# A down projection's first half in 98 block products instead of 112, with the inner factors made by GpSimd

## The chip, the cores and the metric

The kernel runs on one core of a Trainium2 chip. The core has a matrix engine (TensorE, "PE" in the profile; its weight loads are "PEld"), VectorE ("DVE"), ScalarE ("ACT"), GpSimd ("POOL") and SyncE ("SP"), which here issues nearly all DMAs. Each engine works through its own queue in order; the queues meet at semaphores. Matmuls write to PSUM, which VectorE and ScalarE can read and GpSimd in this kernel never touches. The metric is the device time of one execution in microseconds, as a median of several runs.

## What is computed

The input `x` has 8 sequences of 512 tokens of 512 features. All arithmetic is float32.

```
xn = layernorm(x)
q, k, v = xn Wq' + bq, xn Wk' + bk, xn Wv' + bv
s = ((elu(q)+1) * cumsum_over_tokens((elu(k)+1) * v) / sqrt(32)) Wo' + bo
h = silu(xn' Wgate' * scale) * (xn' Wup' * scale)     # xn' = Hadamard transform of xn * SU_ug
f = (Hadamard transform of h * SU_dp) Wdown' * scale   # 2048 -> 512
out = x + s * silu(f)
```

The Hadamard transforms and scales are folded into the weights at the start of the kernel.

## The kernel before

**Pairs, units, halves.** Sequences are taken two at a time (four pairs, p = 0 to 3). The two sequences of a pair are the two rows of a 2x2 block matrix product, and every projection is done with seven block products in place of eight (the Winograd form of Strassen's scheme). The seven factors are called P1 to P7 in the code; each operand tile has an axis of seven places for them. A pair runs attention (q, k, v and the output projection "o"), then the hidden layer in four units (u = 0 to 3, each giving a tile `ho` of 2x128 hidden features by 7 factors by 512 tokens), and after units 1 and 3 one half of the down projection: `down(p, 0, ...)` (units 0 and 1) and `down(p, 1, ...)` (units 2 and 3, which also gates and writes the output).

**Two levels in the hidden layer, one in down.** From the last unit of pair 0 on, the hidden units use the scheme twice (`by_blocks`, L947): for each of seven outer factors, `block_product` (L678) runs seven inner products, each of two matmuls of a 128x128 weight block with 256 tokens, into the PSUM banks px, py and pz. The outer sums a, v, u1, u3 and r are put together by VectorE and ScalarE as they read PSUM, and by two GpSimd additions (L961, L965). The down half has one level: `token_groups` (L568) makes 7 factors x 2 groups of rows x 2 blocks of 128 tokens x 4 contraction tiles, 112 products of 128 tokens with 256 output features.

**Closing a unit.** `gated` (L985) applies SiLU with ScalarE to the gate half, multiplies by the up half into `ho`, and forms the factors P4, P5, P6 and P7 for the next layer. In the units before a down half (`last`), the products for P7 and P2 and their subtractions are on VectorE, otherwise on GpSimd.

**Order.** The program's order is laid out by hand. `at(place, fn)` puts a step on an agenda in which one place is one product of a few matmuls; `advance` runs it. A block product takes its steps at places 0 (P1), 2 (P2), 3 (P7), 4 (P6), 8 (P5), 12 (P3), 13 (P4), and the next outer product begins at place 7, so two are always interleaved. Background work (normalizing later inputs, making weight factors) is put in with `later` and spread by `pace` behind evictions. A scheduler then fixes each engine's order at build time, by this order and by when it expects operands and buffers; `keep_in_program_order` pins an instruction behind the one that was written before it on its engine.

**Buffers.** `t8` has six tiles of 8 KB a partition for results, `hop` two for `ho` and `co`, `wpool` four for weights (asked for three ahead by `get_w`), and `xin` one tile for inputs, for reading normalized tokens back (`squares`) and for weight factors in the making. PSUM has three banks px, one py, two pz and two "t". `factors_kv` (L440) makes two-level factors of Wk and Wv for pairs 2 and 3, in `t8` tiles, during unit 1 of pair 1 and the down half behind it.

Of the kernel before, what the change touches and what calls it, by code (L numbers as in the profile page):

```python
# [8 lines left out]
F32 = mybir.dt.float32  # L9
# [6 lines left out]


P1, P2, P7, P3, P4, P5, P6 = range(7)


@with_exitstack
def kernel(
# [57 lines left out]
        tc.cur_priority = at  # L80

    nearest, urgent, idle = [], [], []

# [255 lines left out]
    def stream_w(name):  # L341
        w = new_w("%s_%s" % (name[0], name[1] if type(name[1]) is int else "%d_%d" % name[1]))
        if name[0] == "gu":
            u, i = name[1]
            nc.sync.dma_start(w, inner[u][:, i])
        elif name[0] == "kv":
            nc.sync.dma_start(w, inner["kv"][:, name[1]])
        elif name[0] == "down":
            h, i = name[1]
            assert wd_made[h] == 4  # L350
            w = by_factor(w, 4)
            nc.sync.dma_start(w, wd[h][:, i])
        else:
            nc.sync.dma_start(flat(w), kept["%s_%d" % name])
            if name[0] == "o":
                w = by_factor(w)
        return w
# [82 lines left out]
    def factors_kv(m, lo, hi):  # L440

        n = hi - lo
        if "kv" not in inner:
            inner["kv"] = dram.tile([P, 7, 2, 7, P], F32, tag="d_kv", name="d_kv")
        d = inner["kv"][:, lo:hi, ("k", "v").index(m)]
        t = t8.tile([P, 4, 4, P], F32, tag="t", name=f"f_{m}_{lo}")
        for g in range(2):
            nc.sync.dma_start(
                t[:, 2 * g : 2 * g + 2, :n],
                kept[f"{m}_{g}"].rearrange("p (j s e) -> p j s e", j=2, s=7)[:, :, lo:hi],  # L450
            )

        def store(c, o):
            nc.sync.dma_start(d[:, :, c, :], t[:, o, :n])

        def plain():
            for c, o in ((P4, 3), (P1, 0), (P2, 1)):
                store(c, o)

        def made(c, o, x, y, op):  # L460
            nc.vector.tensor_tensor(t[:, o, :n], t[:, x, :n], t[:, y, :n], op)
            store(c, o)

        def make():
            for c, o, x, y, op in (
                (P5, 3, 2, 3, ALU.add), (P7, 2, 0, 2, ALU.subtract),
                (P6, 0, 3, 0, ALU.subtract), (P3, 1, 1, 0, ALU.subtract),
            ):
                later(0.7, made, c, o, x, y, op)

        at(8, plain)
        at(14, make)


    agenda = []
# [199 lines left out]
        between()  # L675


    def block_product(name, w, x, out, add, done, time=0):  # L678


        px, py, pz = (bank(t, name, 2) for t in ("px", "py", "pz"))
        sums = {}

        def product(p, i, first):
            for lane in range(2):
                nc.tensor.matmul(  # L686
                    p[:, lane], w[:, lane, i, :], x[:, i, :],
                    start=(first and lane == 0), stop=True, skip_group_check=True,
                )

        def read(what, m, q):
            s = snap.tile([P, 2, H], F32, tag="s", name=f"{what}_{name}")
            if add is None:
                nc.scalar.copy(s, px)
            else:
                nc.vector.tensor_tensor(s, px, add[:, m, :, q], ALU.add)  # L696
            return s

        def output(o, s, p):
            pace(nc.vector.tensor_tensor(o, s, p, ALU.add), time if add is None else time / 2)  # L700

        def p1():
            product(px, P1, True)
            sums["a"] = read("sa", 0, 0)

        def p2():
            product(py, P2, True)
            output(out[:, 0, :, 0], sums["a"], py)

        def p7():  # L710
            product(pz, P7, True)

        def p6():
            product(px, P6, False)
            sums["b"] = read("sb", 1, 0)

        def p5():
            product(px, P5, False)
            sums["c"] = read("sc", 1, 1)
            output(out[:, 1, :, 1], sums["c"], pz)  # L720

        def p3():
            product(px, P3, False)
            if add is None:
                nc.scalar.copy(out[:, 0, :, 1], px)
            else:
                nc.vector.tensor_tensor(out[:, 0, :, 1], px, add[:, 0, :, 1], ALU.add)  # L727

        def p4():
            product(pz, P4, False)  # L730
            output(out[:, 1, :, 0], sums["b"], pz)
            if done:
                done()

        for place, fn in ((0, p1), (2, p2), (3, p7), (4, p6), (8, p5), (12, p3), (13, p4)):
            at(place, fn)
        advance(7)
# [147 lines left out]

    def fetch(name):
        t = t8.tile([P, NT, D], F32, tag="t", name=name)
        nc.sync.dma_start(t.rearrange("p n d -> p (n d)"), kept[name])
        return t


# [55 lines left out]
    def by_blocks(p, name, xo, weights, got, time=0):  # L947

        def new(what):
            return t8.tile([P, 2, 2, 2, H], F32, tag="t", name=f"{what}_{p}_{name}")  # L950

        def outer(i, out, add=None, done=None):
            block_product(f"{name}_{p}_{i}", weights(i), xo[:, i], out, add, done, time)

        ra = new("a")
        rest = {}

        def with_u1():
            rest["u3"] = r = new("u3")
            for m in range(2):  # L960
                nc.gpsimd.tensor_tensor(r[:, m], ru1[:, m], rv[:, m], ALU.add)  # L961

        def with_r():
            for m in range(2):
                nc.gpsimd.tensor_tensor(rv[:, m], rv[:, m], rr[:, m], ALU.add)  # L965
            got(rv, 1, 1)

        outer(P1, ra)
        rv, ru1 = new("v"), new("u1")
        outer(P5, rv)  # L970
        outer(P6, ru1, ra, with_u1)
        outer(P2, ra, ra, lambda: got(ra, 0, 0))
        rr = new("r")
        outer(P7, rr, ru1, with_r)
        while "u3" not in rest:
            advance(1)
        outer(P3, rest["u3"], rest["u3"], lambda: got(rest["u3"], 0, 1))
        outer(P4, ru1, rr, lambda: got(ru1, 1, 0))

    def hidden_unit(p, u, xo, ho, get_w, last, time=0):  # L980

        def sub(eng, c, a, b):
            eng.tensor_tensor(ho[:, :, c], ho[:, :, a], ho[:, :, b], ALU.subtract)  # L983

        def gated(t, a, s):  # L985
            eng = nc.vector if last and a != s else nc.gpsimd
            g, v = (t[:, :, lane].rearrange("p m q t -> p m (q t)") for lane in range(2))
            for m in range(2):
                nc.scalar.activation(g[:, m], g[:, m], AF.Silu, scale=col("w_gate", u + m * NU + a * NG))  # L989
            place = (P1, P7, P2, P3)[2 * a + s]  # L990
            eng.tensor_tensor(ho[:, :, place], g, v, ALU.mult)
            if place == P7:
                sub(eng, P5, P7, P1)
                sub(eng, P6, P3, P5)
                sub(eng, P7, P3, P7)
            if place == P2:
                sub(eng, P4, P2, P6)
# [3 lines left out]
    def down(p, half, hos, get_w, ds=None, ss=None, ys=None):  # L1001
# [43 lines left out]
        if half == 0:  # L1045
            for s in range(2):
                put_by(f"d_{p}_{s}", ds[s])

    def load_y(p, s):
        y = t8.tile([P, NT, D], F32, tag="t", name=f"y_{p}_{s}")  # L1050
# [169 lines left out]
    for p in range(B // 2):  # L1220
# [5 lines left out]
        for u in range(NU):  # L1226
# [5 lines left out]
                at_o = len(queue) - (2 if p == 0 else 0)  # L1232
                queue[at_o:at_o] = [(p, "o", 0), (p, "o", 1)]
            if u % 2:
                queue += [(p, "down", (u // 2, i)) for i in (P1, P7, P2, P6, P5, P3, P4)]
    ahead = []

    def ask(n):
# [107 lines left out]
    for p in range(B // 2):  # L1346
        if p:
            catch_up()
            inner_tokens(xo)
            co = hop.tile([P, 2, 7, L], F32, tag="h", name=f"co_{p}")  # L1350
        heads_made = (attention if p < 2 else attention_by_blocks)(p, xo, co, get_w)
        more = p + 1 < B // 2
        hos = []
        for u in range(NU):
# [9 lines left out]
            else:  # L1364
# [5 lines left out]
                    with background():  # L1370
                        normalized(3)
                ho = hop.tile([P, 2, 7, L], F32, tag="h", name=f"ho_{p}_{u}")
                hidden_unit(p, u, xo, ho, get_w, u % 2 == 1, 1.1 if p > 1 and u == 0 else 0)
                if u == 0:
                    heads_made()
                    project_out(p, co, get_w)
            hos.append(ho)
            late = 1 if p else 0
            if more and late <= u < 2 + late and (p, u) != (0, 1):
                with background():  # L1380
                    normalized(2 * p + 2 + u - late)
            if u == 1:
                if p == 0:
                    weights_ahead(NU - 1)
                    inner_tokens(xo, 6)
                if p == 1:
                    for i, (m, lo, hi) in enumerate((("k", 0, 4), ("k", 4, 7), ("v", 0, 4), ("v", 4, 7))):
                        at(2 + 12 * i, lambda m=m, lo=lo, hi=hi: factors_kv(m, lo, hi))
                flush()
                down(p, 0, hos, get_w)  # L1390
                hos = []
        flush()
        ds = [fetch(f"d_{p}_{s}") for s in range(2)]
        if more:
            catch_up()
# [57 lines left out]
```

## Time and profile before

| | |
|---|---|
| median of 3 runs | 1538.2 us (1536.04 to 1538.99) |
| the profiled execution | 1536.37 us, its span 1534.5 us, mean granted clock 0.997 |
| TensorE busy | 1513.9 us, 6092 records |
| VectorE / ScalarE / GpSimd busy | 1046.2 / 414.7 / 360.5 us |
| DMA | 288.93 MB, mean 188 GB/s |
| first down half of pairs 1, 2, 3 (start to end) | 627.96 to 678.89, 986.5 to 1037.5, 1344 to 1395 us |

A float32 matmul stands as two records in the trace, one behind the other, and their shown lengths overlap; what it costs is read from the distance of starts. "L584" is line 584 of the kernel. A line with shapes reads out<-in, and xN is the count. In a timeline, the bracket at the end of a line gives how long the engine sat idle before it and what ended that.

### The profile page before, as it was taken

How to read it: one execution, taken by the hardware profiler on the slowest of the kernel's cores; microseconds unless marked ns; L12 is line 12 of the kernel's file. 1: busy time of each engine (PE TensorE's matmuls, PEld its weight loads, DVE VectorE, ACT ScalarE, POOL GpSimd, SP SyncE). 2: the span in 40 equal slices, each digit the busy share in tenths (PEclk: the TensorE clock that was granted, in tenths of full speed). 3: DMA queues.
4: the chain of work that ended last, by engine and by line, in shares of the span. 5: the costliest groups of instructions: out<-in, count | busy, mean ns of one | idle time of the engine just before them, and what ended most of it. 6: DMA issues, size and time to landing. Idle time of an engine off the chain costs nothing.

```text
span 1534.5 us, 16212 instructions
## 1 busy us (share of the span) xinstructions
PE 1513.9 (99%) x6092; PEld 1154.2 (75%) x6092; DVE 1046.2 (68%) x1571; ACT 414.7 (27%) x668; POOL 360.5 (23%) x188
## 2 busy tenths in 40 slices
PE   7999999999999999999999999999999999999998
PEld 3446546747874688888885888888886888888887
DVE  8999788469777665636767895715675697633673
ACT  4462341232125411112115232111212332111211
POOL 1000000000320261205511235302621128200631
PEclk9999999999999999999999999999999999999999
DMA  8345778798975244784586644335484443525462
GB/s 275 96 149 170 237 273 238 228 300 280 271 282 141 96 145 176 239 275 164 167 269 217 188 144 162 116 119 182 172 247 154 142 144 113 185 93 183 160 259 81
DMA packets 213726, 288.93 MB, mean 188 GB/s; under 512 B 57488, under 2 KB 169360, under 8 KB 209424
## 3 DMA queue, kind: packets, MB, share of 16 engines
q1 hardware_dynamic: 213504, 287.87, 58.7%
q8 instruction: 48, 0.79, 0.2%
q14 instruction: 30, 0.25, 0.1%
q10 hardware_dynamic: 144, 0.03, 0.0%
HBM read 205.42 MB, written 82.44 MB: 188 GB/s over the span
## 4 chain that ended last, share of the span: by engine, by line
PE 82%; DVE 11%; DMA 4%; issue 1%; ACT 1%; POOL 0%; SPq 0%; POOLq 0%; DVEq 0%; ACTq 0%
PE px_gu L686 17%; PE px_dn L584 12%; PE pz_gu L686 9%; PE pz_dn L584 6%; PE py_gu L686 4%; PE py_dn L584 4%; PE px_kv L686 3%; PE px_o L584 3%; PE px_q L508 3%; PE px_gate L508 2%; PE pz_o L584 2%; PE pz_kv L686 2%; PE pz_q L508 2%; PE px_k L508 1%; PE px_v L508 1%
## 5 line engine op out<-in xcount | busy, mean ns | idle before, releaser
L686 PE MATMUL px_gu<-xo,w_gu 128*128 128x256 f32 x1456 | 348.4, 380 | 0.7 <-DVE sa_gu L696 0.6
L686 PEld LDWEIGHTS px_gu<-xo,w_gu 128*128 128x128 f32 x1456 | 275.2, 190 | 44.3 <-issue 2.4
L961 POOL TENSOR_TENSOR u_gu<-u_gu,v_gu 128x1024 f32<-128x1024 f32 x26 | 61.2, 2376 | 753.0 <-DVE u_gu L727 697.5
L584 PE MATMUL px_dn<-w_down,ho 128*128 128x256 f32 x1024 | 228.8, 379 | 0.9 <-DVE ho L93 0.9
L584 PEld LDWEIGHTS px_dn<-w_down,ho 128*128 128x128 f32 x1024 | 194.5, 190 | 29.4 <-issue 1.9
L686 PE MATMUL pz_gu<-xo,w_gu 128*128 128x256 f32 x728 | 187.4, 380 | 0.5 <-DVE u L524 0.4
L686 PEld LDWEIGHTS pz_gu<-xo,w_gu 128*128 128x128 f32 x728 | 137.6, 190 | 21.2 <-DVE a_gu L700 0.9
L584 PE MATMUL pz_dn<-w_down,ho 128*128 128x256 f32 x496 | 112.5, 379 | 0.6 <-DVE u L524 0.6
L584 PEld LDWEIGHTS pz_dn<-w_down,ho 128*128 128x128 f32 x496 | 93.8, 190 | 15.4 <-issue 1.2
L686 PE MATMUL py_gu<-xo,w_gu 128*128 128x256 f32 x364 | 93.7, 379 | 0.0
L1018 POOL TENSOR_TENSOR s<-s,d 128x512 f32<-128x512 f32 x30 | 40.0, 1332 | 166.0 <-ACT d L1017 166.0
L686 PEld LDWEIGHTS py_gu<-xo,w_gu 128*128 128x128 f32 x364 | 69.2, 190 | 9.4
L965 POOL TENSOR_TENSOR v_gu<-v_gu,r_gu 128x1024 f32<-128x1024 f32 x26 | 60.8, 2361 | 22.8 <-DVE r_gu L727 22.8
L508 PE MATMUL px_q<-xo,w_q 128*128 128x512 f32 x128 | 59.8, 593 | 0.3 <-ACT sa_q L520 0.3
L584 PE MATMUL px_o<-w_o,co 128*128 128x256 f32 x256 | 59.2, 380 | 0.3 <-DVE sa_o L595 0.3
L1017 ACT ACTIVATE d<-d 128x512 f32<-128x512 f32 x31 | 19.5, 630 | 144.9 <-DVE d L599 124.7
L584 PE MATMUL py_dn<-w_down,ho 128*128 128x256 f32 x256 | 57.9, 379 | 0.0
L989 ACT ACTIVATE a_gu<-a_gu,cols_sb 128x512 f32<-128x512 f32 x26 | 18.6, 720 | 142.2 <-DVE a_gu L727 140.8
L983 POOL TENSOR_TENSOR ho<-ho 128x1024 f32<-128x1024 f32 x24 | 56.3, 2357 | 1.4
L584 PEld LDWEIGHTS px_o<-w_o,co 128*128 128x128 f32 x256 | 48.3, 190 | 8.9 <-issue 1.0
L989 ACT ACTIVATE u_gu<-u_gu,cols_sb 128x512 f32<-128x512 f32 x52 | 36.6, 719 | 67.8 <-DVE u_gu L727 64.9
L584 PEld LDWEIGHTS py_dn<-w_down,ho 128*128 128x128 f32 x256 | 48.6, 190 | 6.6
(322 smaller groups left out, 2403.5 us busy)
## 6 DMA issues: line engine op xcount, KB each, us to landing
w_gu<-d_gu SPq DMA_DIRECT2D x91, 896.0 KB, 4.5
w_down<-d_down SPq DMA_DIRECT2D x56, 512.0 KB, 4.6
w_kv<-d_kv SPq DMA_DIRECT2D x14, 896.0 KB, 4.6
d_s<-o SPq DMA_DIRECT2D x8, 1024.0 KB, 6.3
d_d<-dn SPq DMA_DIRECT2D x8, 1024.0 KB, 7.4
d<-d_d SPq DMA_DIRECT2D x8, 1024.0 KB, 5.7
s<-d_s SPq DMA_DIRECT2D x8, 1024.0 KB, 8.7
y<-in_x_dram SPq DMA_DIRECT2D x8, 1024.0 KB, 7.6
```

What stands on the lines that cost most here:

```text
L508: nc.tensor.matmul(p.rearrange("p a t -> p (a t)") if len(r.shape) == 2 else p, ws[k][:, i, :], r, start=(first and k == 0), stop=(k == n ...
L584: nc.tensor.matmul(p[:, c], t[:, (2 * g + c) * P : (2 * g + c + 1) * P], ws[i](k), start=(first and k == 0 and c == cs[0]), stop=(k == n - ...
L686: nc.tensor.matmul(p[:, lane], w[:, lane, i, :], x[:, i, :], start=(first and lane == 0), stop=True, skip_group_check=True,)
L961: nc.gpsimd.tensor_tensor(r[:, m], ru1[:, m], rv[:, m], ALU.add)
L965: nc.gpsimd.tensor_tensor(rv[:, m], rv[:, m], rr[:, m], ALU.add)
L983: eng.tensor_tensor(ho[:, :, c], ho[:, :, a], ho[:, :, b], ALU.subtract)
L989: nc.scalar.activation(g[:, m], g[:, m], AF.Silu, scale=col("w_gate", u + m * NU + a * NG))
L1017: nc.scalar.activation(d, d, AF.Silu)
L1018: (nc.vector if final and (a, s) == (1, 0) else nc.gpsimd).tensor_tensor(r, r, d, ALU.mult)
```

## The change

For pairs 1, 2 and 3 the first half of down is done with two levels as well (`down_by_blocks`). Each of the seven outer factors now has seven inner products, and each of these adds two matmuls (the two feature blocks m of a unit) of a 128x128 weight block with 256 tokens: 7 x 7 x 2 = 98 products. Units 0 and 1 form the two rows of the inner contraction, the token halves its columns. The result comes out with features on partitions.

- The weights need a second level of factors: `factors_down` makes them once, in pair 1's attention, through the `xin` tile into DRAM (`dl`, 896 KB for each outer factor). `factors_kv` moves from unit 1 to places 118 to 163 of pair 1 and takes the `xin` tile too; the normalizing of sequences 4 and 5 moves to the beginning of pair 1.
- The inner factors of the activations are made by GpSimd: for each outer factor three subtractions on 128x512 (`factors`) and one after the P2 product (`last_factor`), all pinned to the written order. The first two sets begin in `gated` as soon as P3 is there.
- In the units before a down half, SiLU's result for P7 and P2 goes to a PSUM bank "t", and VectorE multiplies and subtracts from there, in 128x512 pieces; P6 and P4 go to GpSimd.
- The results are turned in 32x32 blocks by VectorE into the tile of unit 1's `ho` and stored as [token, feature] in eight DMAs a pair, four places apart (`store`), in runs of 32 elements. `fetch` reads that layout.

```
+    def factors_down(i):
+        if "dl" not in inner:
+            inner["dl"] = dram.tile([P, 7, 2, 7, P], F32, tag="d_dl", name="d_dl")
+        t = xin.tile([P, 3, 7, P], F32, tag="x", name=f"f_dl_{i}")
+        w = t.rearrange("p c s e -> p (c s e)")[:, : 2 * 7 * P].rearrange("p (m s e) -> p m s e", m=2, s=7)
+        for c in range(2):
+            for u in range(2):
+                nc.sync.dma_start(
+                    w[:, :, (P1, P2, P7, P4)[2 * c + u]], wd[0][:, i, 2 * u : 2 * u + 2, c * P : (c + 1) * P]
+                )
...
+                later(0.42, nc.vector.tensor_tensor, w[:, :, o], w[:, :, a], w[:, :, b], op)
...
+    def two_terms(w, x):
+        def product(p, i, first):
+            for k in range(2):
+                nc.tensor.matmul(
+                    p[:, 0], w[:, k, i, :], x(k, i),
+                    start=(first and k == 0), stop=(k == 1), skip_group_check=True,
+                )
+        return product
...
         def gated(t, a, s):
-            eng = nc.vector if last and a != s else nc.gpsimd
+            eng = nc.gpsimd
             g, v = (t[:, :, lane].rearrange("p m q t -> p m (q t)") for lane in range(2))
+            if last and a != s:
+                bs = []
+                for m in range(2):
+                    b = bank("t", f"g_{p}_{u}_{a}_{m}", 1)[:, 0]
+                    nc.scalar.activation(b, g[:, m], AF.Silu, scale=col("w_gate", u + m * NU + a * NG))
+                    if s:
+                        nc.vector.tensor_tensor(b, b, v[:, m], ALU.mult)
+                        nc.vector.tensor_tensor(ho[:, m, P5], b, ho[:, m, P1], ALU.subtract)
+                        bs.append(b)
+                    else:
+                        nc.vector.tensor_tensor(ho[:, m, P2], b, v[:, m], ALU.mult)
+                if s:
+                    in_order(sub(eng, P6, P3, P5))
+                    for m in range(2):
+                        nc.vector.tensor_tensor(ho[:, m, P7], ho[:, m, P3], bs[m], ALU.subtract)
+                else:
+                    in_order(sub(eng, P4, P2, P6))
+                return
...
+            if begin and place == P3:
+                begin()
...
+    def down_by_blocks(p, hos, get_w):
...
+        ORDER = (P1, P3, P6, P5, P7, P2, P4)
+        def factors(n):
...
+            in_order(nc.gpsimd.tensor_tensor(x, b(1, 1, o), b(0, 1, o), ALU.subtract))
+            in_order(nc.gpsimd.tensor_tensor(b(0, 1, o), b(0, 1, o), b(0, 0, o), ALU.subtract))
+            in_order(nc.gpsimd.tensor_tensor(y, b(1, 1, o), b(0, 1, o), ALU.subtract))
+            places[n] = {
+                P1: b(0, 0, o), P2: b(1, 0, o), P7: x, P6: y, P5: b(0, 1, o), P3: b(1, 1, o), P4: b(1, 0, o)
+            }
+        def last_factor(n):
+            b = block(1, 0, ORDER[n])
+            in_order(nc.gpsimd.tensor_tensor(b, b, places[n][P6], ALU.subtract))
...
+        def store(s, place):
+            z = h1[:, s, 0:4].rearrange("p c (i f) -> p c i f", f=32)
+            d = ds[s].rearrange("(i t) (c j f) -> j t c i f", t=32, j=4, f=32)
+            for j in range(4):
+                at(place + 4 * j, lambda j=j: nc.sync.dma_start(d[j], z[32 * j : 32 * j + 32]))
...
+        def begin():
+            room.extend(halves("r3"))
+            factors(0)
+            room.extend(halves("xy"))
+            factors(1)
+        def run():
+            at(4, lambda: factors(2))
+            for n in range(3, 7):
+                at(7 * n - 7, lambda n=n: factors(n))
+            for n in range(7):
+                at(7 * n + 3, lambda n=n: last_factor(n))
...
+            def plus(o, a, b):
+                o, a, b = (t.rearrange("p m l q t -> p (m l q t)") for t in (o, a, b))
+                nc.vector.tensor_tensor(o, a, b, ALU.add)
...
+            if p == 1:
+                with background():
+                    for b in (4, 5):
+                        normalized(b)
+                for n, i in enumerate(IN_TURN):
+                    at(40 + 11 * n, lambda i=i: factors_down(i))
+                for i, (m, lo, hi) in enumerate((("k", 0, 4), ("k", 4, 7), ("v", 0, 4), ("v", 4, 7))):
+                    at(118 + 15 * i, lambda m=m, lo=lo, hi=hi: factors_kv(m, lo, hi))
...
-                down(p, 0, hos, get_w)
+                if p:
+                    down_now()
+                else:
+                    down(p, 0, hos, get_w)
```

## The prediction

> **What bounds the kernel now.** I read the page's busy row first, then the chain, then the stage that the change rewrites, engine by engine.
>
> ```profile
> PE 1513.9 (99%) x6092; PEld 1154.2 (75%) x6092; DVE 1046.2 (68%) x1571; ACT 414.7 (27%) x668; POOL 360.5 (23%) x188
> PE 82%; DVE 11%; DMA 4%; issue 1%; ACT 1%; POOL 0%; SPq 0%; POOLq 0%; DVEq 0%; ACTq 0%
> ```
>
> TensorE is busy 99% of the span and carries 82% of the chain; GpSimd (POOL) is idle 77% of it. So time goes only if matmuls go, and comes back only where TensorE is made to wait. Next, a table by stretches over the first down half of pairs 1, 2 and 3, and TensorE's timeline in the first of them:
>
> ```profile
> 627.96:678.89 50.93, 50.93 (x237) 44.78 (x236) 21.88 (x31) 7.46 (x12) 2.00 (x1) 1.00 0.76 236
> 986.50:1037.50 51.00, 51.00 (x238) 44.82 (x237) 13.88 (x17) 7.46 (x12) 2.07 (x1) 1.00 0.39 125
> 1344.00:1395.00 51.00, 51.00 (x238) 44.80 (x238) 14.30 (x17) 7.50 (x13) 2.38 (x1) 1.00 0.38 119
> ...
> 635.73 1.46 PE L584 MATMUL px_dn<-w_down,ho 128*128 128x256 f32 x6
> 637.02 1.89 PE L584 MATMUL pz_dn<-w_down,ho 128*128 128x256 f32 x8
> 638.75 2.32 PE L584 MATMUL px_dn<-w_down,ho 128*128 128x256 f32 x10
> ...
> 654.72 17.43 PE L584 MATMUL px_dn<-w_down,ho 128*128 128x256 f32 x80
> 671.99 7.07 PE L584 MATMUL pz_dn<-w_down,ho 128*128 128x256 f32 x32
> ```
>
> The columns after the stretch are its length, then busy time (and count) of PE, PEld, DVE, ACT, POOL, then granted clock (1.00), DMA share and GB/s. All three stretches run TensorE without a gap; GpSimd has one instruction. A product leaves two records; the 80 records start 17.27 us before the next line, so a record is worth 17.27 / 80 = 0.216 us and a product 0.432 us. (The 380 ns of the page's groups overlap.) The three short lines show a second thing: six records of P1 run ahead of eight of P7 and the rest of P1 after them. The written order has P7's first. Whatever fixes TensorE's order at build time fills an expected wait with later work.
>
> GpSimd just before that stage, and its price for 512 elements:
>
> ```profile
> 622.09 4.68 POOL L965 TENSOR_TENSOR v_gu<-v_gu,r_gu 128x1024 f32<-128x1024 f32 x2 [2.13 <-DVE r_gu L727]
> 627.59 2.36 POOL L991 TENSOR_TENSOR ho<-v_gu 128x1024 f32<-128x1024 f32 x1 [0.83 <-ACT v_gu L989]
> ...
> L1018 POOL TENSOR_TENSOR s<-s,d x30: 1262/1267/1638, 419.3 to 1524.4; 128x512 f32<-128x512 f32 x30
> ...
> L991 DVE TENSOR_TENSOR ho<-u_gu x14: 1224/1312/1423, 399.3 to 1487.2; 128x1024 f32<-128x1024 f32 x14
> L983 DVE TENSOR_TENSOR ho<-ho x28: 1206/1212/1226, 400.8 to 1488.5; 128x1024 f32<-128x1024 f32 x28
> ```
>
> The reader should see that GpSimd is free from 629.95 on, that an operation on 128x512 takes 1.27 us (three figures: least, median, most), and that VectorE does twice the elements in 1.21 us.
>
> **The change part by part.**
>
> *Matmuls removed.* Now: 7 factors x 4 row blocks x 4 contraction tiles = 112 products, 48.4 us a pair. After: 7 outer x 7 inner x 2 terms = 98 of the same shape, 42.3 us. That is 14 x 0.432 = 6.04 us a pair, 18.1 us for three.
>
> *GpSimd's factors.* Each outer product needs four operations on 128x512: three in factors(), one in last_factor(). 28 x 1.27 = 35.5 us a pair, 5.07 us per outer product, against 14 x 0.432 = 6.04 us of TensorE. It keeps up by 0.97 us an outer product once it is ahead; the question is the start. Write a place as one product of two matmuls, 0.863 us, with place 0 at 627.96. Pinned order: the P3 product ends at 629.95; factors(0) gives x, the changed block and y at 631.2, 632.5 and 633.8. The first outer product wants x at place 3 (630.6) and y at place 4 (631.4): TensorE, if it kept the written order, would lose 0.7 and 1.7 us. factors(1) ends 637.6; P6, now on GpSimd, takes 2.36, to 639.9; last_factor(0) 641.2, wanted at 641.6 with the loss so far. factors(2) 645.0; P4, also moved, 647.4; last_factor(1) 648.6, wanted at place 20, 645.2 + 2.4 = 647.6: 1.1 more. factors(3) ends 652.4 against a want of 653.0, and from there GpSimd gains. So 3.5 us a pair is the most for the written order. Zero is the least: behind the first wait stand three products that need none of this (the last two of the unit and the next outer P1), 2.6 us, and the px6-pz8-px10 lines show such work being drawn forward. That row concerns a VectorE wait, though, and none shows a TensorE wait on GpSimd, so I take 1.5 us a pair, a little under the middle: 4.5 us.
>
> *VectorE against GpSimd.* Among new VectorE work only three additions (plus) per pair read two SBUF tensors; the gated products read PSUM. The row for L991 shows what an overlap costs: 1.40 us at 629.63, beside a GpSimd instruction, against 1.22 at 637.64. GpSimd's own L1018 goes from 1.27 to at most 1.64. Three additions of 1.22 us would hold GpSimd up by at most 3.7 us, after the third outer product, when it is 0.6 to 3.4 us ahead: 0 to 0.5 us a pair, taken as 0. [...]
>
> *The other VectorE work.* Per pair 37 evictions of 128x256 at 0.42 us (the L307 row's 419 ns), three additions at 1.22 and eight transposes at 0.68: 24.6 us (the whole stretch has 14 to 22 now, the unit's tail included). TensorE's 42 us covers it, and each PSUM bank is read with four places (3.45 us) to spare. P6 and P4 leave VectorE.
>
> *The gated products through PSUM, fourth unit too.* Activations 1.44 us, then six VectorE steps of 0.68 in place of 1.40 + 1.21 + 2.35: P7 is ready near 636 as now, and the early P1 and P7 products over the older unit cover it to 640.9. P4 would be ready at 641.3 and is wanted at 672. Nothing, up to 1 us a pair if that cover shrank.
>
> *Weights.* Seven loads of 896 KB for seven of 512 KB; the hidden units already take one 896 KB load (4.4 us) per 6.04 us. Nothing.
>
> *Stores.* Four transposes per token block, then eight stores of 256 KB in runs of 128 bytes, SP issuing them in turn with later weight loads behind, over 31 places (27 us) of the third unit. Nothing of before stores in such runs. The nearest row is the load z of the same shape: 4.0/6.1/7.7 us to land, and in the packet records 13 ns a packet alone, 20 in bursts. At 20 the 16,384 packets hold 16 engines 20 us, beside 15 us of work already there (DMA share 0.57 to 0.67 over 26 us): 35 us in 27, so loads slip up to 8 us. Weights are asked for three outer products ahead, 18.1 − 4.4 = 13.7 us of slack. Taken as nothing; it turns at 25 to 26 ns a packet. [...]
>
> *Pair 1's preparations.* Seven times, during attention: four loads of 128 KB, four VectorE operations at 0.42 and a store of 896 KB, all through the one xin buffer, with four factors_kv chains and two normalizations brought forward behind the same buffer. VectorE is busy 53 of 78 us there; 12 us of factors and one normalization (6 us) fit. A chain is about 4 + 2 + 6 us; five to seven end near 570 to 600, wanted from about 610. Bounds 0 to 4 us (SP or VectorE standing before a late buffer); I take 1, plus 0.3 a pair where halves join: 2.
>
> Sum: −18.1 + 4.5 + 2 = −11.6. Against the profiled execution (1536.37 = span 1534.5 + 1.87) that is 1524.8; the median of the three runs is 1.8 higher, so 1526.6. I say 1526.5.
>
> **Rivals.**
> *Everything is filled* (no wait survives): 1538.2 − 18.1 = 1520. For it, the gapless stretches; against, the zero margin at places 3, 4 and 20.
> *Most is lost in small waits*: written order kept (10.5), the VectorE additions (1.5) and 4 for pair 1: −2, so 1536; within 0.2% or just under.
> *GpSimd becomes the bound*, slower: it must do 28 operations and 4.72 us from 629.95. The old half ended at 678.9; with 1 us for the last product it decides at (678.9 − 629.95 − 4.7 − 1) / 28 = 1.54 us an operation. At 1.64, the most in the L1018 row, it ends 2.7 us later than now, 8 in all, 1546; with additions in the way 1552. Against: the median 1.27, and few two-input VectorE instructions nearby.
> *The 128-byte stores make weights late*, slower, if a packet takes over 28 ns: at 32, 33 + 15 − 27 − 13.7 = 7 us a pair, 1538.2 − 11.6 + 21 = 1548.
>
> **How the numbers follow.** Forecast 0.48 (its own range 1522 to 1532), filled 0.15, lost in waits 0.13, GpSimd 0.12, stores or late preparations 0.12. A measurement tells about 0.2%, 3 us, from no change. Faster: 0.48 + 0.15 + 0.08 = 0.71; same 0.05; slower 0.24. The range runs from 1519 (below the filled case) to 1543, leaving out the worse part of the two slow cases, some 0.17, and a little below.
>
> **What would show it.** The dl products in place of the dn ones: 196 records and 42.3 us a pair. Gaps on TensorE at the first px6 or pz7 and second pz4 of a dl stage, released by GpSimd, up to 3.5 us. GpSimd over 85% busy in that stage, its 128x512 median at 1.27; above 1.54 I am wrong about the sign. Stores landing in 6 us and gu weights still 4 to 5 us. If gaps stand instead around 480 to 620, the xin chain is the cause.

## Result and profile after

The changed kernel takes 1549.8 us (median), the kernel before 1537.1 in the same series: a ratio of 1.0085, 95% interval 1.0065 to 1.0105. The change makes the kernel slower, by 12.7 us; the forecast was 11.6 us faster. One execution of the changed kernel took 2264 us at a mean clock of 0.656 and is left out here, but not in the 1550.8 us from which the expectations below start. The profiled execution took 1549.79 us, its span 1548.0.

The page's busy row and the shares of the chain, of the changed kernel:

```profile
PE 1503.6 (97%) x6008; PEld 1140.0 (74%) x6008; DVE 1113.2 (72%) x1739; ACT 413.9 (27%) x680; POOL 508.9 (33%) x286
PE 78%; DVE 10%; POOL 4%; DMA 3%; issue 2%; ACT 1%; SPq 1%; POOLq 0%; DVEq 0%; ACTq 0%
```

84 records of TensorE are gone, which at 0.216 us is the promised 18.1 us. But TensorE fell from 99% to 97% of the span, and GpSimd, which had no share of the chain, has 4% of it. So the answer is in TensorE's waits. I counted them from the trace: wherever the start of one matmul follows the start of the one before by more than the 0.216 us of a 256-column record (0.432 for 512 columns), the excess is time in which TensorE stood or ran at a lower clock. The sum was 19.5 us before and is 51.4 now. 31.9 more, less 18.1, is 13.8; the span grew by 13.5. Where the excess lies:

```
excess over back-to-back matmuls, us
                              before   after
pair 1, 500 to 600 us           0.5      9.1   (one gap at 572)
pair 1, 600 to 650              0.0     10.4   (one gap at 611; start of the down half)
pair 1, 650 to 700              0.1      4.3   (down half)
pair 2's down half              0.2      5.6
pair 3's down half              0.0      4.3
all else                       18.7     17.7
```

Half of the loss lies before the rewritten products, in the stretch where the new weight factors are prepared. TensorE's waits from 555 to 620 us of the changed kernel (line, what it waited for: us in total, times, longest):

```profile
PE pz_gu L717 <- DVE u_gu L747: 5.6, 1, 5.6
PE px_gu L717 <- DMA w_gu<-d_gu: 5.3, 1, 5.3
```

The first, at 572.56, is a wait for an eviction on VectorE. Here is what VectorE did with the factors of Wd in that time, and below it GpSimd (start, duration, then the operation):

```profile
562.39 2.06 DVE L97 TENSOR_TENSOR f_dl<-f_dl 128x256 f32<-128x256 f32 x1
564.98 6.93 DVE L97 TENSOR_TENSOR f_dl<-f_dl 128x256 f32<-128x256 f32 x3
582.35 1.55 DVE L97 TENSOR_TENSOR f_dl<-f_dl 128x256 f32<-128x256 f32 x4
```
```profile
559.50 2.37 POOL L1057 TENSOR_TENSOR ho<-v_gu 128x1024 f32<-128x1024 f32 x1 [0.83 <-ACT v_gu L1055]
561.82 2.36 POOL L1057 TENSOR_TENSOR ho<-u_gu 128x1024 f32<-128x1024 f32 x1
564.25 7.37 POOL L1031 TENSOR_TENSOR ho<-ho 128x1024 f32<-128x1024 f32 x3
```

Seven sets of four small operations make these factors. The last set, from 582.35, does four in 1.55 us, beside no work of GpSimd. The four of the set before it take 2.06 us and three times 2.3 on average, a whole GpSimd operation each: while GpSimd ran one 2.36 us operation on two SBUF tensors behind another, each of these VectorE operations with two SBUF inputs got through once for one of GpSimd's. The eviction that TensorE needs is behind them in VectorE's queue.

The second gap, at 611.25, is a wait for a weight load. TensorE wanted the weights at 605.8; SP issued the load at 603.71, and it landed 7.5 us later instead of the usual 4.7. Here is SP's queue ahead of the load, and a table by stretches of the changed kernel (length, then busy time and count of PE, PEld, DVE, ACT, POOL, then granted clock, DMA share and GB/s):

```profile
596.88 3.01 SPq L462 DMA_DIRECT2D d_kv<-f_k  x4
599.93 0.54 SPq L930 DMA_DIRECT2D d_s<-o  x1
602.26 1.36 SPq L456 DMA_DIRECT2D f_k<-d_k  x2
603.71 0.59 SPq L349 DMA_DIRECT2D w_gu<-d_gu  x1
```
```profile
600.00:605.00 5.00, 5.00 (x25) 4.41 (x24) 1.29 (x2) 2.22 (x4) 0.00 (x0) 1.00 0.98 331
605.00:612.00 7.00, 1.71 (x7) 1.17 (x6) 0.72 (x2) 0.58 (x1) 0.00 (x0) 0.79 1.01 337
```

Two things come together. SP stood before stores of `factors_kv` (L462), whose VectorE steps were not done (2.8 us at the longest), and its next loads (L456, 1.7 us in two waits), and the weight load is behind them in its queue. And the DMA engines are full (shares of 0.98 and 1.01): results of attention, the stores and loads of `factors_kv` and weight loads share them. With the usual 4.7 us the load would have landed at 608.4, still 2.6 us late. The clock column shows a third thing: 0.79. After each of the two gaps TensorE's records start 0.427 us apart instead of 0.216, for 12 records after the first and 9 after the second. With that the gap at 572 costs 8.7 us (5.8 stood, 2.9 behind it) and the one at 611 7.8 (5.4 and 2.4).

The down halves themselves, in TensorE's timeline of pair 1 (the bracket is the idle time before, and what ended it):

```profile
646.25 1.13 PE L726 MATMUL pz_dl<-r_dl,w_dl 128*128 128x256 f32 x4 [0.53 <-POOL r_dl L1144]
648.95 1.13 PE L726 MATMUL px_dl<-r_dl,w_dl 128*128 128x256 f32 x4 [1.56 <-POOL r_dl L1146]
...
658.13 1.10 PE L726 MATMUL pz_dl<-ho,w_dl 128*128 128x256 f32 x4 [0.72 <-DVE a_dl L747]
...
665.42 1.13 PE L726 MATMUL pz_dl<-ho,w_dl 128*128 128x256 f32 x4 [1.44 <-POOL ho L1153]
```

From start to start, TensorE lost 0.69 and 1.73 us at the first two products that need a factor of GpSimd's, the same in all three pairs. The later two waits are pair 1's own: there the operations of `factors_kv` on VectorE run beside GpSimd's too, and both sides lose. A step of `factors_kv` (L469) took 2.24 us at 654.22, with the eviction for 658.13 behind it; GpSimd's timeline at that time is

```profile
653.10 2.81 POOL L1031 TENSOR_TENSOR ho<-ho 128x1024 f32<-128x1024 f32 x1
655.87 1.73 POOL L1153 TENSOR_TENSOR ho<-ho,r_dl 128x512 f32<-128x512 f32 x1
```

These and the operations at 650.20 and 658.90 (1.60 each) are 1.6 us longer together than 2.36 and 1.27 each, as much as the wait at 665.42.

A table by stretches of pairs 1 and 2, then operations of the down half with the least, median and most ns, then loads and stores of the page's last part (KB each, median us to landing):

```profile
639.74:684.00 44.26, 39.23 (x176) 32.56 (x174) 31.43 (x48) 8.29 (x18) 42.49 (x28) 1.00 0.67 208
998.00:1042.50 44.50, 41.69 (x182) 35.16 (x181) 24.23 (x43) 8.53 (x18) 42.65 (x30) 0.96 0.42 142
```
```profile
L1144 POOL TENSOR_TENSOR r_dl<-ho,ho x3: 1262/1262/1272, 644.9 to 1361.6; 128x512 f32<-128x512 f32 x3
L1197 DVE TENSOR_TENSOR r_dl<-r_dl,a_dl x3: 1237/1467/1870, 680.5 to 1394.3; 128x1024 f32<-128x1024 f32 x3
L1197 DVE TENSOR_TENSOR r_dl<-r_dl,u_dl x3: 1950/1954/1955, 682.0 to 1396.0; 128x1024 f32<-128x1024 f32 x3
```
```profile
w_gu<-d_gu SPq DMA_DIRECT2D x91, 896.0 KB, 4.7
w_dl<-d_dl SPq DMA_DIRECT2D x21, 896.0 KB, 4.6
d_d<-ho SPq DMA_DIRECT2D x24, 256.0 KB, 6.2
```

GpSimd is 96% busy, an undisturbed operation takes the 1.27 us foreseen, and weights and stores land in 4.6 and 6.2 us.

### The profile page after: what moved, and what is told of

It is laid out like the page before. It is cut to its first block, busy times and chain, and to the rows that moved or that the text cites. A ratio compares the mean times of both kernels' runs of the same rounds, so it can differ in the third digit from the quotient of the medians.

```text
span 1548.0 us, 16497 instructions
## 1 busy us (share of the span) xinstructions
PE 1503.6 (97%) x6008; PEld 1140.0 (74%) x6008; DVE 1113.2 (72%) x1739; ACT 413.9 (27%) x680; POOL 508.9 (33%) x286
## 4 chain that ended last, share of the span: by engine, by line
PE 78%; DVE 10%; POOL 4%; DMA 3%; issue 2%; ACT 1%; SPq 1%; POOLq 0%; DVEq 0%; ACTq 0%
PE px_gu L717 16%; PE pz_gu L717 8%; PE px_dn L620 8%; PE py_gu L717 4%; PE pz_dn L620 4%; PE px_o L620 3%; PE px_kv L717 3%; PE px_dl L726 3%; PE px_q L544 3%; PE px_gate L544 2%; PE py_dn L620 2%; PE px_up L544 2%; PE pz_o L620 2%; PE pz_kv L717 2%; PE pz_dl L726 2%
## 5 line engine op out<-in xcount | busy, mean ns | idle before, releaser
L620 PE MATMUL px_dn<-w_down,ho 128*128 128x256 f32 x640 | 143.0, 379 | 1.0 <-DVE ho L97 1.0
L620 PEld LDWEIGHTS px_dn<-w_down,ho 128*128 128x128 f32 x640 | 121.5, 190 | 19.6 <-issue 1.9
L1031 POOL TENSOR_TENSOR ho<-ho 128x1024 f32<-128x1024 f32 x38 | 90.0, 2375 | 25.0 <-DVE ho L1046 14.7
L726 PE MATMUL px_dl<-ho,w_dl 128*128 128x256 f32 x300 | 74.6, 385 | 1.5 <-DVE sc_dl L743 1.0
L620 PE MATMUL pz_dn<-w_down,ho 128*128 128x256 f32 x304 | 69.3, 380 | 0.3 <-DVE u L560 0.3
L726 PEld LDWEIGHTS px_dl<-ho,w_dl 128*128 128x128 f32 x300 | 57.6, 193 | 11.1 <-DVE sc_dl L743 2.3
L620 PEld LDWEIGHTS pz_dn<-w_down,ho 128*128 128x128 f32 x304 | 57.4, 190 | 10.6 <-issue 1.2
L1085 ACT ACTIVATE d<-d 128x512 f32<-128x512 f32 x31 | 19.5, 630 | 147.0 <-DVE d L635 127.3
L717 PE MATMUL px_kv<-xo,w_kv 128*128 128x256 f32 x224 | 53.6, 379 | 0.0
```

Of the source, the lines that this page charges most:

```text
L620: nc.tensor.matmul(p[:, c], t[:, (2 * g + c) * P : (2 * g + c + 1) * P], ws[i](k), start=(first and k == 0 and c == cs[0]), stop=(k == n - ...
L717: nc.tensor.matmul(p[:, lane], w[:, lane, i, :], x[:, i, :], start=(first and lane == 0), stop=True, skip_group_check=True,)
L726: nc.tensor.matmul(p[:, 0], w[:, k, i, :], x(k, i), start=(first and k == 0), stop=(k == 1), skip_group_check=True,)
L1031: return eng.tensor_tensor(ho[:, :, c], ho[:, :, a], ho[:, :, b], ALU.subtract)
L1085: nc.scalar.activation(d, d, AF.Silu)
```

## The experiments

The theory after the result: matmuls went as foreseen, and three separate things took more than they gave: (a) operations on VectorE with two SBUF inputs wait for GpSimd, which costs the gap at 572; (b) full DMA engines, which cost the gap at 611 (the runs below show another cause); (c) GpSimd's first factors come too late in each pair. The rivals: the gap at 572 is VectorE having too much to do at that place; (c) is hidden elsewhere; and the two large parts of the change, products through PSUM and factors on GpSimd, are themselves the loss. All edits are made on the changed kernel. It takes 1549.8 us; each series has its own runs of the kernel before, 1536.1 to 1537.3.

**encode_psum: one operand of each encode step through PSUM.**

```diff
+            nc.scalar.copy(b[:, 0], w[:, :, P4])
+            nc.scalar.copy(b[:, 1], w[:, :, P1])
-                later(0.42, nc.vector.tensor_tensor, w[:, :, o], w[:, :, a], w[:, :, b], op)
+            later(0.42, tt, w[:, :, P5], w[:, :, P7], b[:, 0], ALU.add)
...
```

> Only the seven encodes of the dl weights change: ScalarE first copies one operand of each subtraction to a PSUM bank, so that no VectorE instruction of them reads two SBUF tensors; place, count and sizes stay. Theory (GpSimd and a VectorE instruction with two SBUF inputs exclude each other): the f_dl instructions at 562 to 572 us fall from 2.0 to 2.6 us each to about 0.42, the 5.8 us gap of TensorE at 572 and the 2.9 us of slow matmuls behind it go, 1550.8 - 8.7 = about 1542. Rival (the set is simply late, by its loads or its place in VectorE's order): the instructions wait instead of lasting, the gap stays within 1 us, 1549 to 1552.

1545.3 us (1.0067, 1.0041 to 1.0093). The same number of VectorE operations, at about the same places; the set that made the gap stands at 567.00 to 569.61, beside GpSimd operations of 2.36 us as before. One of the two groups of the tile f_dl:

```profile
L97 DVE TENSOR_TENSOR f_dl<-t_e_dl,f_dl x14: 406/412/424, 497.7 to 581.1; 128x256 f32<-128x256 f32 x14
```

The longest is 424 ns, where the changed kernel has 2558. The gap at 572 is gone: from 500 to 600 us the excess is 1.0 instead of 9.1. That is (a), and not VectorE's load, since VectorE does the same work. The median fell by 4.5 us only, and the two intervals overlap, so the cause is shown by the trace and not by the time. Of the difference, 3.2 us are excess before 500 us, all of it ahead of the first instruction that differs (480 us). That is spread between executions, not a cost of the edit: over all the profiles here the excess ahead of 400 us varies by 3.9 us. The late weight load is still there, with a wait of 6.0 us.

**kv_moved: `factors_kv` later, out of the crowded stretch.**

```diff
-                for i, (m, lo, hi) in enumerate((("k", 0, 4), ("k", 4, 7), ("v", 0, 4), ("v", 4, 7))):
-                    at(118 + 15 * i, lambda m=m, lo=lo, hi=hi: factors_kv(m, lo, hi))
+                for i, (m, lo, hi) in zip((166, 182, 262, 280), (("k", 0, 4), ("k", 4, 7), ("v", 0, 4), ("v", 4, 7))):
+                    at(i, lambda m=m, lo=lo, hi=hi: factors_kv(m, lo, hi))
```

Its four steps are also issued one a place (`at(j, ...)`) in place of `later(0.7, ...)`.

> Only factors_kv moves: its four sets begin at places 166, 182, 262 and 280 of pair 1 in place of 118, 133, 148 and 163, and their VectorE work is issued at once, not behind evictions. Theory (the DMA engines are full at 590 to 612 us, with stores of o, stores of kv factors and loads of weights together, and a gu weight comes late): the 5.4 us gap at 611 and the 2.5 us of slow matmuls behind it go, and in pair 1's dl stage the waits beyond those of pair 2 (about 2 to 3 us) go: about 1540. Rival (the weight is late because SP stands before the xin buffer that the dl factors hold): the gap stays or moves by no more than 2 us, 1548 to 1552.

1553.4 us (1.0114, 1.0092 to 1.0137): a miss for the time. The table by stretches, and VectorE a little later:

```profile
600.00:605.00 5.00, 5.00 (x25) 4.24 (x24) 1.30 (x3) 1.76 (x3) 0.00 (x0) 1.00 1.02 348
```
```profile
635.57 2.10 DVE L469 TENSOR_TENSOR f_k<-f_k 128x384 f32<-128x384 f32 x1
637.59 0.68 DVE L743 TENSOR_TENSOR sc_gu<-px_gu,u_gu 128x512 f32<-128x512 f32 x1
638.20 2.65 DVE L469 TENSOR_TENSOR f_k<-f_k 128x384 f32<-128x384 f32 x1
```

TensorE has no gap around 611, so the gap comes from `factors_kv`. But (b) does not hold: the DMA engines are as full as before (1.02), and the two weight loads that SP issued at 598.60 and 599.09 took 6.7 and 8.4 us to land. What changed is the time of issue: 1.3 us after the first product behind the output projection, against 8.35 us in the changed kernel. Two of the kernels below say the same. This is how long the weight load took that TensorE waited for near that place, and the wait, in early_first and then in all_fixed (where the DMA share is 1.00 from 590 to 605):

```profile
DMA to landing us min/median/max: 5.9/5.9/5.9
PE px_gu L717 <- DMA w_gu<-d_gu: 3.9, 1, 3.9
```
```profile
DMA to landing us min/median/max: 9.4/9.4/9.4
PE px_gu L725 <- DMA w_gu<-d_gu: 1.0, 1, 1.0
```

A load that lands in 5.9 us is waited for when it is issued late, at 605.30; one that needs 9.4 us, issued at 592.74, costs 1.0. The gap at 611 is SP's queue standing before `factors_kv`; the full DMA engines only lengthen it.

Nor is time gained, for the moved operations now stand beside GpSimd, take 2.10 and 2.65 us in place of 0.55, and TensorE waits three times behind them, 4.8 us in all from 634 to 641. One wait was exchanged for another of kind (a).

**early_first: the first factors behind the unit's P1 product.**

```diff
-            if begin and place == P3:
-                begin()
+            if begin and place in (P1, P3):
+                begin((P1, P3).index(place))
...
+                elif begin:
+                    at(16, lambda: in_order(sub(eng, P4, P2, P6)))
```

`factors(0)` is given to GpSimd before the P3 product, `factors(1)` behind it. The subtraction that makes P4 is put off 16 places, and there it reads a P6 that its own last factor has already replaced: the P4 factor of this kernel, and of all_three, is another one than the reference's. Instructions and sizes are the same, so the time can be read.

> The first three GpSimd operations of a dl stage are written behind the P1 product instead of the P3 product, and the P4 subtraction sixteen places later. Theory (TensorE waits for x, y and the last factor only because GpSimd begins too late): the waits of 0.7 and 1.7 us at the first dl products go in all three pairs, with the slow matmuls behind them in pair 2: 2.5 to 4 us a pair, about 1541. Rival (GpSimd is the bound of the stage in any order): the wait moves to a later factor, and the time stays within 3 us of 1550.8.

1545.5 us (1.0065, 1.0040 to 1.0089). In pairs 2 and 3 the excess of the down half falls from 5.6 and 4.3 us to 2.5 each; the two waits on GpSimd are gone. What is left in pair 2:

```profile
PE px_dl L726 <- DVE sc_dl L743: 0.9, 1, 0.9
PE px_gu L717 <- DVE sc_gu L743: 0.8, 1, 0.8
```

The second stands behind the six gating operations on VectorE, the first behind an addition of two SBUF tensors (L1197), which takes 2.0 us beside GpSimd. So (c) holds, with 1.8 to 3.1 us a pair; the time, 4.3 us less, lies between theory and rival.

**gate_sbuf and factors_vector: each of the change's two large parts undone alone.**

```diff
-            eng = nc.gpsimd
+            eng = nc.vector if last and a != s else nc.gpsimd
...
-            if last and a != s:
+            if False:
```

> The changed kernel with one part undone: the gated products for P7 and P2 and their subtractions are on VectorE in SBUF, as in the kernel before. Theory of exclusion: six VectorE instructions a pair with two SBUF inputs now meet GpSimd's unbroken row of factors, each stands up to 1.3 to 2.4 us, and the evictions behind them are late: 3 to 6 us a pair, about 1560 to 1568. Rival (it is GpSimd's own load that counts, which loses 4.7 us a pair here): the first waits of the dl stage shrink, 1543 to 1548.

1559.3 us (1.0150, 1.0133 to 1.0167), with products and subtractions on SBUF tensors. The start of pair 2's down half, GpSimd, and what TensorE waits for:

```profile
1007.90 2.25 POOL L1144 TENSOR_TENSOR r_dl<-ho,ho 128x512 f32<-128x512 f32 x1
1010.22 2.13 POOL L1145 TENSOR_TENSOR ho<-ho 128x512 f32<-128x512 f32 x1
1012.43 2.12 POOL L1146 TENSOR_TENSOR r_dl<-ho,ho 128x512 f32<-128x512 f32 x1
```
```profile
PE px_dl L726 <- POOL r_dl L1146: 3.3, 1, 3.3
PE pz_dl L726 <- POOL r_dl L1144: 1.8, 1, 1.8
```

GpSimd's factors take 2.1 to 2.25 us in place of 1.27, and both starting waits grow. This part as a whole (PSUM, and P6 and P4 on GpSimd) is worth 9.6 us to the changed kernel.

```diff
-            in_order(nc.gpsimd.tensor_tensor(x, b(1, 1, o), b(0, 1, o), ALU.subtract))
+            in_order(nc.vector.tensor_tensor(x, b(1, 1, o), b(0, 1, o), ALU.subtract))
...
```

The other two and `last_factor` go to VectorE likewise.

> The changed kernel with the 28 operations of factors and last_factor on VectorE in place of GpSimd (P6 and P4 stay on GpSimd). If VectorE's load bounds the stage: 28 x 0.69 = 19.3 us on top of the 24.6 and the gating, some 50 us for 42 us of matmuls, 6 us or more a pair later, 1565 to 1575. Rival (VectorE does an operation in half the time, and nothing excludes anything): the waits for x, y and the last factor go and little replaces them, 1540 to 1546.

1567.7 us (1.0198, 1.0176 to 1.0219). VectorE is 40.0 of 44.5 us busy in pair 2's down half, against 24.2, and the waits move to its evictions:

```profile
PE pz_gu L717 <- DVE u_gu L747: 2.6, 1, 2.6
```

So neither large part is the loss; each is better as the change has it.

**all_three: the first three edits together.**

> The three edits together. If the three causes are separate and make up the loss, the gains add: 1550.8 - 8.7 - 11 - 9 = about 1522, below the kernel before. If they hide one another or a common limit stands behind them, less than two thirds of that, above 1532.

1541.2 us (1.0027, 1.0013 to 1.0040): better than each alone, and above what adding them up gave, since `factors_kv` at its new place brings its waits along (12.1 us of excess from 600 to 650, of it 5.3 in three waits from 631 to 641). That is the second of the two readings foreseen, above 1532.

**all_fixed: the steps of `factors_kv` through PSUM too, at places 258, 278, 298 and 318.** Here the P4 subtraction is put off by 9 places, ahead of the last factor.

```diff
+            nc.scalar.copy(b, t[:, 3, :n])
+            nc.scalar.copy(b2, t[:, 0, :n])
+            made(P5, 3, t[:, 2, :n], b, ALU.add)
...
+                    at(9, lambda: in_order(sub(eng, P4, P2, P6)))
```

> Three edits on the changed kernel: the encodes of the dl weights through PSUM; the four sets of factors_kv at places 258, 278, 298 and 318 of pair 1 (its third and fourth unit), their operands too through PSUM; the first three GpSimd operations of a dl stage behind the P1 product and the P4 subtraction nine places later, before the last factor of P6. Theory (exclusion of two-SBUF-input VectorE work and GpSimd, full DMA engines at 590 to 612, a late start of GpSimd): the gaps at 572 and 611 us go (-16), pair 1's dl stage waits no longer than the others, and 2.5 us a pair stay: 1550.8 - 16 - 4 - 5 = about 1526, below the kernel before. Rival (the preparations cost wherever they stand): the waits turn up at 680 to 760 us, and the time stays above 1534.

1533.7 us (0.9976, 0.9966 to 0.9986): faster than before, by 3.6 us, though not the 11 hoped for. The excess is 34.6 us, 15.1 over that of before: 0.7 from 500 to 600 us, 5.1 from 600 to 700, 2.6 and 2.5 in pairs 2 and 3, 2.2 from 700 to 850, and 3.1 more than the kernel before ahead of 500 us, which is no more than the spread between executions. In pair 1's down half three waits of 1.0, 0.8 and 0.8 us are left, all behind evictions on VectorE.

**all_plus: the additions (`plus`) as well, in halves with one operand through PSUM.**

```diff
-                nc.vector.tensor_tensor(o, a, b, ALU.add)
+                for m in range(2):
+                    nc.scalar.copy(c, b[:, m])
+                    nc.vector.tensor_tensor(o[:, m], a[:, m], c, ALU.add)
```

> all_fixed, and the three additions of a dl stage (plus) in halves of 512 whose second operand ScalarE has copied to PSUM. Theory of exclusion: the additions, 2.0 us each beside GpSimd in place of 1.22, fall to two of about 0.7, and the wait of 1.0 us late in each dl stage goes: 2 to 3 us below all_fixed. Rival (more instructions, more waits): the same or up to 2 us above it.

1540.3 us (1.0024, 1.0012 to 1.0036): a miss. In pairs 2 and 3 the excess fell as foreseen, 2.6 to 1.4. But in pair 1 a gap of 8.2 us opened at 725, in the hidden units behind the down half. SP's waits from 690 to 730 us, its timeline there, and TensorE's wait for weights from 550 to 780:

```profile
SPq L462 <- DVE f_k L469: 11.1, 2, 10.9
```
```profile
705.92 0.58 SPq L1177 DMA_DIRECT2D d_d<-ho  x1
717.45 2.15 SPq L462 DMA_DIRECT2D d_kv<-f_k  x4
719.68 0.47 SPq L349 DMA_DIRECT2D w_gu<-d_gu  x1
```
```profile
PE px_gu L725 <- DMA w_gu<-d_gu: 10.7, 3, 8.0
```

SP stood 10.9 us before a store of `factors_kv` whose VectorE step had not run, and a weight load was behind it in SP's queue: the same kind of gap as the one at 611 of the changed kernel. The next three kernels ask what that gap hangs on.

**best_paced, best_moved: the steps of `factors_kv` given room between evictions again; its four starts moved to 268, 286, 304 and 322.**

```diff
-            made(P5, 3, t[:, 2, :n], b, ALU.add)
+            later(0.7, made, P5, 3, t[:, 2, :n], b, ALU.add)
...
```

The other three steps likewise, and evictions in the third and fourth units of pair 1 are given such room; that is best_paced. best_moved changes the four places alone.

> All_plus (1540.3), with the encode steps of the attention weights given out one behind each eviction (room 0.7 us) instead of all at once, and with such room in units 3 and 4 of pair 1. Theory 'queue': the 8.2 and 2.2 us gaps at 725 to 740 come from SP standing 10.9 us before a store whose VectorE step was late, with the weight loads behind it; a step with room no longer piles up, but a store can still stand, so the sum stays uncertain: if the piling up was the cause, the gap goes and the time is 1528 to 1532. Rival 'late wherever': paced steps come later still, SP stands longer before their stores, and the gap stays or grows: 1540 or more.

> All_plus (1540.3), with the four preparations of the attention weights begun at places 268, 286, 304 and 322 instead of 258, 278, 298 and 318; nothing else changes. Theory 'queue': SP's wait before the store depends on where the VectorE step falls among evictions, gating and additions; 10 places (8.6 us) later for the first and 4 for the last move the last two further into the stage of pair 1 that has the additions, so a wait of SP comes again, of the size of the last one: 1536 to 1544. Rival 'position only': the gap was a chance meeting of one store with one weight load, and goes: 1529 to 1532.

1546.2 us (1.0061, 1.0044 to 1.0078) and 1541.9 (1.0030, 1.0018 to 1.0043). In both, SP stands before such a store again (6.7 and 7.4 us at the longest) and TensorE before a weight load for 6.4 and 7.5. Neither pacing nor a shift of 4 to 10 places cures it, as the rival of the first text and the theory of the second had said.

**plus_late: all_plus with pair 1's additions whole again.**

```diff
+                if p == 1:
+                    nc.vector.tensor_tensor(o, a, b, ALU.add)
+                    return
```

> All_plus with the additions of pair 1 back as one VectorE operation on two SBUF tensors each; the halves through PSUM stay in pairs 2 and 3. Pair 1 is then as in all_fixed (1533.7), whose SP had no wait over 5.1 us there, and pairs 2 and 3 lose 1.35 us each instead of 2.5. Theory 'the additions cost their own wait, and the 8 us of all_plus belong to pair 1 alone': 1533.7 - 2 x 1.15 = 1531.4. Rival 'the ScalarE copies of the halves cost somewhere of their own, in every pair': 1534 or more.

1530.3 us (0.9957, 0.9943 to 0.9971): the best of all, 5.8 us under the kernel before, and 1.1 under what was expected. The excess from 700 to 850 us is 1.6 instead of 18.0. So the gap belongs to the halved additions of pair 1 together with `factors_kv`; by which step of the planner they hold up the VectorE operation is open. Pair 1 pays for the whole additions with one wait of 2.0 us.

## Why the prediction was wrong

The forecast for the profiled execution was 1524.8 us, and it took 1549.8: 25 us to explain. By the terms of the sum:

- **Matmuls removed**, −18.1: exact, 6008 records for 6092.
- **Pair 1's preparations**, bounded 0 to 4 and taken as 2 with the joins: this step failed. The gaps at 572 and 611 cost 8.7 and 7.8 us. The step counted how long VectorE and the chain through xin would be busy, and that held (the 28 operations had all begun by 583.5 us). It did not ask which engine would run beside those operations; encode_psum shows that the gap at 572 was their two SBUF inputs. The gap at 611 is what the step itself named, "SP or VectorE standing before a late buffer", but its price was too low: SP stood before `factors_kv` while a weight load was behind it, and the slow clock came on top. So "the xin chain is the cause" was wrong for the first gap and near the truth for the second.
- **VectorE against GpSimd**, 0 to 0.5 a pair and taken as 0: this step failed too, in size and in reach. The row for L991 showed a loss of 0.18 us, where 0.32 us of the operations overlapped. The profile of before had a row with nearly the whole price that the forecast did not weigh; it stands below the list. Where GpSimd ran without a pause, VectorE operations with two SBUF inputs lost far more: 0.42 us became 2.0 to 2.6 beside GpSimd operations of 2.36, and the additions took 1.95 (L1197) against 1.22. With one operand in PSUM they took 406 to 424 ns beside the same operations of GpSimd (encode_psum). The forecast also counted only the three additions; the operations of factors_down and factors_kv, which are of the same kind, cost more.
- **GpSimd's factors**, 0 to 3.5 a pair and taken as 1.5: the working was right, the choice was not. It gave 0.7 and 1.7 us for the written order, and the trace has 0.69 and 1.73 in every pair; nothing was drawn forward into them. The third wait, 1.1 at last_factor(1), did not come in pairs 2 and 3; in pair 1 it was 1.6, by VectorE's disturbance. With 0.1 us behind each wait and 1.7 us of lower clock in pair 2, the starts cost 9.6 us for three pairs in place of 4.5. The row with px6, pz8 and px10 showed TensorE's work filled around a VectorE wait and was carried over to a wait on GpSimd, which no row showed.
- The rest of the down halves, 7.0 us in place of 0, is mostly evictions and factors behind such pairs of operations: 4.2 in pair 1, where `factors_kv` runs, 1.1 and 1.7 in the others.
- **Stores, weights, the products through PSUM, the GpSimd price**: right. 256 KB in runs of 128 bytes landed in 6.2 us, at 13 ns a packet (the forecast gives two turning points for one thing, 25 to 26 and 28 ns; the packet is far under both), weights in 4.6 and 4.7, and no weight load was late in pairs 2 and 3.

The row for VectorE against GpSimd, GpSimd's operation and VectorE's beside it in the profile of before:

```profile
529.39 2.19 POOL L315 TENSOR_TENSOR co<-co 128x512 f32<-128x512 f32 x1 [28.33 <-DVE co L791]
529.23 1.22 DVE L762 SCALAR_TENSOR_TENSOR q<-q,neg_q 128x1024 f32<-128x1024 f32 x1
```

An operation of 1.27 us (the other one of L315) took 2.19 beside a VectorE operation with two SBUF inputs that had begun just before it: it lost 0.92 us of the 1.06 for which they overlapped.

Together: 14.5 us over the allowance for the preparations, 5.1 at the starts and 7.0 behind them are 26.6, less 1.0 in all the other stages: 25.6 for the 25 to explain.

Of the rivals, the one for late preparations came true. It had no working of its own: the 1548 us were worked out for late stores, so that they lie near the 1549.8 is luck. GpSimd as the bound did not: where it was disturbed it was by VectorE's two-input operations. The mechanism of the forecast holds too: with the costs taken away one by one, the 98 products beat the old half (1530.3 against 1536.1).

## What to carry to other kernels

When work is given to an engine that was idle, list every VectorE instruction with two SBUF inputs in the whole stretch where both run, and price each at the full length of the other's operation (here 0.42 us became 2.0 to 2.6 beside operations of 2.36); with one operand copied to PSUM by an idle ScalarE the same operation took 0.41 (406 to 424 ns). A preparation "that fits" must fit beside its neighbours and in the queue that issues the DMAs, not only on its own engine: a store that waits for a late step holds the weight loads behind it (10.9 us of SP's queue in all_plus, 8.0 of TensorE's time). And a wait that the written order yields stays in the sum until a row shows that kind of wait being filled.

## What the runs showed that I had not expected

- Waits of TensorE cost more than their length in three places. After the waits of 5.8 and 5.4 us the records started 0.427 us apart, 12 and 9 of them, so that 2.9 and 2.4 us came on top. After the same wait of 1.73 us, seven records were slow in pair 2 and none in pairs 1 and 3. The granted clock was 0.50 in the three stretches where they lie, of 6.83, 6.83 and 3.41 us:

```profile
571.51:578.34 6.83, 5.78 (x14) 4.63 (x15) 2.88 (x5) 1.44 (x2) 2.26 (x2) 0.50 0.72 262
609.05:615.88 6.83, 4.63 (x11) 3.75 (x12) 3.84 (x7) 0.00 (x0) 0.00 (x0) 0.50 0.98 310
1008.41:1011.82 3.41, 3.41 (x10) 2.70 (x9) 0.00 (x0) 0.65 (x2) 3.25 (x3) 0.50 0.00 0
```

  In pairs 1 and 3 it stayed at 1.00 through the same two waits, of 0.7 and 1.7 us. So in this kernel the length of a wait did not tell by itself whether slow records follow; nothing here shows what does.
- A repair of one wait often moved another: moving `factors_kv` took the gap of 5.4 us at 611 away and cost 3.6 us more in all, and halving three additions in pair 1 brought a gap of 8.2 us at a place 50 us later, by way of SP's queue.
